# The fifth run of attention scores moved ahead of the output product, in a two-layer kernel on one core

## The chip, the cores and the metric

The kernel runs on one core of a Trainium2 chip. The core has a matrix engine (PE, with its weight loads PEld), a vector engine (DVE), an activation engine (ACT), a general engine (POOL), and a queue that issues transfers (SP). Each engine works through its own instructions in the order in which the program gives them, and semaphores hold an instruction back until what it needs is there. The metric is the time of one execution in microseconds (us), as the device measures it; lower is better.

## The reference, cut to what matters

There are 8 batches of 512 tokens with 256 channels. Each of two layers normalises its input and adds an attention and a feed-forward result to it. The change lies in the first layer's attention, which has 16 heads of 64 channels, rotated queries and keys, and a causal mask:

```python
q = (x @ Wq + bq).reshape(b, s, H, L)      # the same for k and v
q = _apply_rope(q, cos, sin)               # and k
scores = jnp.einsum('bnqd,bnkd->bnqk', q, k) / jnp.sqrt(jnp.float32(L))
scores = jnp.where(causal, scores, -1000000000.0)
attn = jax.nn.softmax(scores, axis=-1)
attended = jnp.einsum('bnqk,bnkd->bnqd', attn, v)
return attended @ Wo + bo
```

The first layer's feed-forward part is a product with eight-bit weights, the second layer an attention with a gate and a feed-forward part with a gate. The change does not touch them.

## The kernel before, in words

**Tiling.** One pass (`at`, 0 to 15) does the attention of eight heads of one batch, so a batch takes two passes: `b, g = divmod(at, 2)`. In this text an even pass has g = 0, an odd pass g = 1. The score matrix of a head is causal; it is cut into 16 strips of 32 query rows, and strip i needs 32 (i + 1) key columns. The strips are grouped into five runs (`RUNS`): run 0 has strips 15, 14 and 0; run 1 has 13, 1, 12, 2; run 2 has 11, 3, 10, 4; run 3 has 9, 5, 8, 6; run 4 has strip 7 alone. A strip pair fills 512 columns of a PSUM bank, and there is one bank for each of two sets of heads. All PSUM tiles come from one pool of eight banks that are given out in rotation.

**What one run goes through.** `scores(at, run)` (L463) makes the score matmuls on tiles of 64 rows by 32 columns of the array (L474). `soften` (L481) has DVE add the mask and take the maximum (L500) and ACT take the exponential with its sum (L504). `divide` (L510) takes reciprocals on DVE (L515) and scales the chances on POOL (L520). `turn` (L528) transposes the chances on DVE (L540). When all five runs are turned, `weigh` (L545) multiplies them with the values (L553) in the next pass, and `keep_weighed` (L561) has ACT copy the result out of PSUM (L567).

**What else a pass does.** `project(at, which)` computes rotated queries (which = 0) or keys (which = 1) of a later pass: matmuls into `pq` (L395) on the whole array, copied out by ACT with the bias (L400), half exchanged by SP's transfers (`y<-l`, L402); `turn_qk` (L405) rotates them later with two DVE products (L412) and a sum on POOL (L427). `project_v` (L429) computes values into `pv` (L437), which ACT copies out (L443) and SP stores. `finish(at - 1)` (L373) is the output product of the pass before, for two halves of the tokens: matmuls into `pw` (L357) on the whole array and an addition on DVE (L366). In even passes 2 to 12, `transpose_x(b + 1)` (L307) transposes the normalised input of the next batch on PE into `pxt` (L313), ACT copies it to `xnT` (L316), and SP stores `xnT` for later (`xnf`, L305) and then loads the input of a later batch (L80). The keys of `project(at + 2, 1)` in an even pass are made from just this new `xnT`. Passes 12 and 13 also do part of the feed-forward product of two batches (`add_quantised`, L193).

**What sets the order.** The order of the work is written out by hand (`manual_schedule`): every engine has its instructions in the order of the calls in the program. The calls of passes 1 to 13 around the change are these (L849 to L869), with the branches for single passes left out:

```python
scores(at, 3); soften(at, 3)
turn_qk(2 * at + 3, 0); turn(at, 2); divide(at, 3)
transpose_x(b + 1)           # even passes
finish(at - 1)
scores(at, 4); soften(at, 4)
turn(at, 3); project(at + 2, 1); divide(at, 4)
```

Behind them the next pass begins with its run 0, `turn(at, 4)` and `weigh(at)`. Pass 14 leaves the loop ahead of these lines.

## Time and profile before

| what | value |
| --- | --- |
| time, median of 3 runs | 960.23 us (958.95 to 961.5) |
| time of the profiled execution | 956.88 us |
| span of the profiled execution | 955.1 us |
| granted clock of PE | 0.996 |
| busy: PE, DVE, POOL, ACT | 98%, 83%, 59%, 55% |
| output product, `pw` (L357) | 512 matmuls, 114.3 us |
| keys, `pq` from `wk` (L395) | 256 matmuls, 116.0 us |
| all scores (L474) | 4096 matmuls, 147.0 us |
| exponential of strip 7 (128 x 256) | 32, 501 ns each |
| maximum of strip 7 (128 x 256) | 32, 417 ns each |
| copies `xnT<-pxt` | 16, 572 ns each |

The profile shows one execution. Rows of a timeline give the start and the duration in microseconds, the engine, the line, the operation, the output and the input by their names in the program, the shapes, and how many instructions were merged in the row; in brackets stands how long the engine had been idle, and what ended the wait. Matmuls are pipelined and their ends are modelled, so that starts are the safer reading. The chain of waits is followed back from the last instruction, so it shows what set the end. "issue" stands for time in which an engine waited for nothing that the profile shows.

### The profile page before, as it was taken

The page shows a single profiled execution, that of the slowest core. Times are in us where ns is not written, and L with a number is a line of the kernel's source. Part 1 is how long each engine was busy: PE and PEld are TensorE (multiplying, and loading weights), DVE is VectorE, ACT ScalarE, POOL GpSimd, SP SyncE. Part 2 cuts the span into 40 slices and gives each one's busy share as a digit, 9 for nine tenths or more (in the row PEclk, how much of TensorE's full clock was granted, in tenths as well). Part 3 has the DMA queues.
Part 4 walks back from the last instruction along what each step waited for, and adds up shares of the span by engine and source line. Part 5 has one row for each costly group of instructions (what it writes and reads, how often), then busy time and mean ns, then how long its engine had stood idle before and what let it go on. Part 6 is the DMA issues. An engine that isn't in the chain of part 4 may idle for free.

```text
span 955.1 us, 27426 instructions
## 1 busy us (share of the span) xinstructions
PE 933.0 (98%) x10491; PEld 595.1 (62%) x10491; DVE 788.4 (83%) x2429; ACT 529.7 (55%) x1480; POOL 563.9 (59%) x698
## 2 busy tenths in 40 slices
PE   9989999999999999999999999999999999999998
PEld 5436555656666575656565655665656677777776
DVE  4898988898799789978997898787989588888864
ACT  3565465656564656574656655555667335555553
POOL 3595775655664757556665665989776424444321
PEclk9999999999999999999999999999999999999999
DMA  7666354426443545254444435353344122221111
GB/s 216 182 177 174 98 128 139 122 73 141 145 107 96 125 131 133 69 135 128 118 109 129 121 89 156 112 156 90 91 123 124 46 76 67 71 69 51 34 33 34
DMA packets 60930, 105.40 MB, mean 110 GB/s; under 512 B 7552, under 2 KB 38272, under 8 KB 60800
## 3 DMA queue, kind: packets, MB, share of 16 engines
q1 hardware_dynamic: 58928, 102.01, 39.4%
q10 hardware_dynamic: 1872, 1.64, 0.7%
q8 instruction: 83, 1.36, 0.6%
q14 instruction: 47, 0.39, 0.1%
HBM read 39.14 MB, written 28.84 MB: 71 GB/s over the span
## 4 chain that ended last, share of the span: by engine, by line
PE 88%; DVE 5%; issue 2%; POOL 2%; ACT 2%; DMA 1%; SPq 0%; DVEq 0%; ACTq 0%; POOLq 0%
PE pq L395 21%; PE av L553 13%; PE sc L474 13%; PE pw L357 11%; PE pv L437 9%; PE po L713 6%; PE pk L660 3%; PE pg L675 3%; PE pvv L687 3%; PE c L632 2%; PE trc L700 1%; PE plr L234 1%; DVE t L540 1%; DVE p L500 1%; POOL h L427 1%
## 5 line engine op out<-in xcount | busy, mean ns | idle before, releaser
L504 ACT ACTIVATE p<-p,nm 128x64 f32<-128x64 f32 (+15 forms) x512 | 260.0, 511 | 154.4 <-DVE nm L500 124.4
L520 POOL TENSOR_SCALAR p<-p,rs 128x64 f32<-128x64 f32 (+15 forms) x512 | 270.1, 548 | 53.5 <-DVE rs L515 51.3
L427 POOL TENSOR_TENSOR h<-h,y 128x1024 f32<-128x1024 f32 x64 | 166.7, 2606 | 178.3 <-DVE y L412 97.0
L500 DVE CUSTOM_DVE_ANT_0 p<-sc,cmask 128x64 f32<-128x64 f32 (+15 forms) x512 | 191.1, 436 | 75.4 <-PE sc L474 74.9
L540 DVE STREAM_TRANSPOSE t<-p 128x256 f32<-128x256 f32 (+3 forms) x640 | 192.7, 367 | 20.7 <-POOL p L520 20.7
L474 PE MATMUL sc<-h,h 64*32 64x416 f32 (+15 forms) x4096 | 147.0, 398 | 9.0 <-issue 5.8
L474 PEld LDWEIGHTS sc<-h,h 64*32 64x32 f32 x4096 | 76.9, 107 | 95.6 <-issue 69.8
L553 PE MATMUL av<-t,vr 32*64 32x96 f32 (+15 forms) x4096 | 128.4, 394 | 2.9 <-issue 2.7
L553 PEld LDWEIGHTS av<-t,vr 32*64 32x64 f32 x4096 | 120.5, 131 | 10.3 <-issue 6.8
L395 PE MATMUL pq<-xnT,wk 128*128 128x512 f32 x256 | 116.0, 605 | 3.6 <-ACT xnT L316 3.6
L400 ACT ACTIVATE l<-pq,cs 128x512 f32<-128x512 f32 x128 | 84.5, 682 | 59.6 <-PE pq L395 54.5
L412 DVE TENSOR_TENSOR y<-y,cs 128x1024 f32<-128x1024 f32 x64 | 111.5, 1743 | 5.6 <-DMA y<-l 5.1
L395 PE MATMUL pq<-xnT,wq 128*128 128x512 f32 x256 | 114.5, 599 | 1.1 <-ACT att L567 0.9
L357 PE MATMUL pw<-wo,att 128*128 128x256 f32 x512 | 114.3, 381 | 0.0
L437 PE MATMUL pv<-wv,xnT 128*128 128x512 f32 x256 | 114.0, 598 | 0.0
L357 PEld LDWEIGHTS pw<-wo,att 128*128 128x128 f32 x512 | 96.0, 190 | 16.0 <-issue 3.7
L504 ACT ACTIVATION_READ_ACCUMULATOR p<-p,nm 128x1 f32 x512 | 96.8, 189 | 0.0
L395 PEld LDWEIGHTS pq<-xnT,wk 128*128 128x128 f32 x256 | 48.1, 192 | 65.0 <-issue 58.3
L437 PEld LDWEIGHTS pv<-wv,xnT 128*128 128x128 f32 x256 | 47.5, 190 | 57.9 <-issue 54.6
L395 PEld LDWEIGHTS pq<-xnT,wq 128*128 128x128 f32 x256 | 47.4, 190 | 56.8 <-issue 47.9
L412 DVE TENSOR_TENSOR h<-l,cs 128x1024 f32<-128x1024 f32 x64 | 78.7, 1230 | 4.3 <-ACT l L400 4.3
L567 ACT ACTIVATE att<-av,cs 128x512 f32<-128x512 f32 x64 | 38.7, 688 | 69.5 <-PE av L553 69.5
(111 smaller groups left out, 955.7 us busy)
## 6 DMA issues: line engine op xcount, KB each, us to landing
y<-l SPq DMA_DIRECT2D x256, 128.0 KB, 2.3
va<-v SPq DMA_DIRECT2D x32, 512.0 KB, 3.0
vr<-va SPq DMA_DIRECT2D x64, 256.0 KB, 4.5
x<-in_x SPq DMA_DIRECT2D x15, 512.0 KB, 4.5
xnf<-xnT SPq DMA_DIRECT2D x8, 512.0 KB, 3.0
x1f<-x SPq DMA_DIRECT2D x7, 512.0 KB, 3.6
out<-y SPq DMA_DIRECT2D x14, 256.0 KB, 2.2
cut_wo<-xnf SPq DMA_DIRECT2D x5, 512.0 KB, 4.5
```

The lines of the kernel that those rows point to most:

```text
L357: nc.tensor.matmul(pw[:, j, :], atts[at, p][:, tok], wo[:, 4 * (at % NH) + p, :], start=(p == 0), stop=(p == 3),)
L395: nc.tensor.matmul(pb, w[:, g, k, bass.ts(t, P)], xnT[b][:, k, :], start=(k == 0), stop=(k == NK - 1),)
L400: nc.scalar.activation(l[:, t, :], pb, AF.Identity, bias=cs[:, bias : bias + 1])
L412: nc.vector.tensor_tensor(dst, src, table[:, None, :].to_broadcast([P, 2, S]), ALU.mult)
L427: nc.gpsimd.tensor_tensor(h, h, y, ALU.add)
L437: nc.tensor.matmul(pb.rearrange("p (g n) -> p g n", g=2), xnT[b][:, k, bass.ts(2 * half + j, P)], wqkv[2][:, 2 * g : 2 * g + 2, k, :], sta ...
L474: nc.tensor.matmul(scored[at, i][e][j * Q : j * Q + Q, :], q[rows, j % 2, bass.ts(i, Q)], k[rows, j % 2, :n], start=True, stop=True,)
L500: nc.vector.tensor_tensor_reduce(p[:, e, col : col + n], sc, cmask[:, S - n :], -1.0 / L**0.5, BIG, ALU.add, ALU.min, nm[:, c : c + 1],)
L504: nc.scalar.activation(p[:, e, col : col + n], p[:, e, col : col + n], AF.Exp, bias=nm[:, c : c + 1], scale=-1.0, accum_out=sm[:, c : c + 1],)
L520: nc.gpsimd.tensor_scalar(p, p, rs[:, c : c + 1], 1.0, ALU.mult, ALU.mult)
L540: nc.vector.transpose(turned[at][c][:, :, at_ : at_ + (n - 1) * pitch(c) + 1 : pitch(c), :], p[:, :, c * P : c * P + n * Q].rearrange("p e ...
L553: nc.tensor.matmul(banks[j][e * L : e * L + L, i * Q :], vs[at][rows, m, c, bass.ts(e, L)], t[c][rows, e, m * pitch(c) + m : m * pitch(c) ...
```

## The change

Run 4 of the scores and its softmax are called ahead of the input's transposes and of the output product, directly behind what follows run 3. So on PE run 4 stands directly behind run 3, and the output product is followed by the keys. On DVE the two maxima of run 4 stand ahead of the two additions of the output product. On ACT the two exponentials of run 4 stand ahead of the two `xnT` copies in even passes. The order on POOL and SP stays. The change reaches passes 1 to 13.

```diff
@@ -851,6 +851,8 @@
             turn_qk(2 * at + 3, 0)
             turn(at, 2)
             divide(at, 3)
+            scores(at, 4)
+            soften(at, 4)
             if g == 0 and b < B - 1:
                 transpose_x(b + 1)
                 if b + 2 < B:
@@ -861,8 +863,6 @@
             finish(at - 1)
             if at == last - 2:
                 first_norm()
-            scores(at, 4)
-            soften(at, 4)
             turn(at, 3)
             if two:
                 project(at + 2, 1)
```

## The prediction

> **What bounds the kernel now.** I read the busy shares and the shares of the chain first, then the chain in order of time, then the timelines of PE, ACT and DVE around the moved step.

> The page's busy times and the chain's shares by engine:

> ```profile
> span 955.1 us, 27426 instructions
> ...
> PE 933.0 (98%) x10491; PEld 595.1 (62%) x10491; DVE 788.4 (83%) x2429; ACT 529.7 (55%) x1480; POOL 563.9 (59%) x698
> ...
> PE 88%; DVE 5%; issue 2%; POOL 2%; ACT 2%; DMA 1%; SPq 0%; DVEq 0%; ACTq 0%; POOLq 0%
> ```

> PE is busy for 98% of the span and carries 88% of the chain; the other engines have room on average (DVE 83%). So a gain is PE time saved in the loop, and a loss is anything that makes PE wait. Two stretches of PE's timeline, one odd pass (at = 3) and one even pass (at = 4); columns are start, duration, engine, line, operation, count:

> ```profile
> 196.90 1.96 PE L474 MATMUL sc<-h,h 64*32 64x320 f32 x64
> 198.78 7.17 PE L357 MATMUL pw<-wo,att 128*128 128x256 f32 x32
> 205.89 0.66 PE L474 MATMUL sc<-h,h 64*32 64x256 f32 x16
> 206.48 7.13 PE L395 MATMUL pq<-xnT,wk 128*128 128x512 f32 x16
> ```

> ```profile
> 241.84 1.96 PE L474 MATMUL sc<-h,h 64*32 64x320 f32 x64
> 243.72 1.09 PE L313 MATMUL pxt<-ident,x 128*128 128x128 f32 x8
> 244.66 7.07 PE L357 MATMUL pw<-wo,att 128*128 128x256 f32 x32
> 251.66 0.66 PE L474 MATMUL sc<-h,h 64*32 64x256 f32 x16
> 252.25 7.13 PE L395 MATMUL pq<-xnT,wk 128*128 128x512 f32 x16
> ```

> The reader sees no gap: each block starts where the one before it stops. I count a block from its start to the next block's start, since the ends are modelled: run 3 takes 1.89 (198.78 - 196.90, rounded), the output product pw 7.10 in the odd pass and 7.00 in the even one, run 4 0.59, the keys pq 7.06. Even passes alone transpose the next batch's input (pxt, 0.93), and their pq reads just that transposed input, xnT, which ACT copies out of PSUM. ACT and DVE in the same even pass:

> ```profile
> 247.57 1.04 ACT L316 COPY xnT<-pxt 128x512 f32<-128x512 f32 x2
> 252.97 0.51 ACT L504 ACTIVATE p<-p,nm 128x256 f32<-128x256 f32 x1 [4.35 <-DVE nm L500]
> ```

> ```profile
> 248.06 2.78 DVE L540 STREAM_TRANSPOSE t<-p 128x256 f32<-128x256 f32 x9
> 250.76 0.20 DVE L515 RECIPROCAL rs<-sm 128x4 f32<-128x4 f32 x2
> 250.88 0.66 DVE L366 TENSOR_TENSOR x<-pw,x 128x512 f32<-128x512 f32 x1
> ...
> 252.44 0.42 DVE L500 CUSTOM_DVE_ANT_0 p<-sc,cmask 128x256 f32<-128x256 f32 x1
> ```

> ACT now makes the two xnT copies at 247.57 and then idles 4.35 for DVE before run 4's exponentials. DVE has no gap between run 3's scores and the reciprocals at 250.76.

> **The change, part by part.** Nothing is added or removed; 16 score matmuls, two DVE maxima, two exponentials and their reads change place in 13 passes (at = 1 to 13). I write times as offsets from the start of run 3's scores.

> *PE, saving.* Run 4 now follows run 3. The trace holds this very pair once, after the loop, where 80 score matmuls stand together, from 703.10 to 705.42:

> ```profile
> 703.10 2.39 PE L474 MATMUL sc<-h,h 64*32 64x320 f32 x80
> 705.42 3.72 PE L357 MATMUL pw<-wo,att 128*128 128x256 f32 x16
> ```

> That is 2.32 against 1.89 + 0.59 = 2.48: 0.16 saved. A full-array block also pays at its edges with a tiled block (scores, av, c). Two rows of the chain in order of time have the same 16 matmuls, once between av and c, once between plr and trc:

> ```profile
> 758.77 3.65 PE pvv L687 x16
> ...
> 795.16 3.45 PE pvv L687 x16
> ```

> That is 0.20 for two edges, 0.10 for one; pw agrees (7.10 entered from scores, 7.00 entered from pxt). The change takes away pw's edge to run 4 and pq's edge from it: 0.20. A pass saves 0.16 + 0.20 = 0.36. Odd pass: 16.64 before, 2.32 + 7.00 + 6.96 = 16.28 after; a pq of 6.96 stands in the trace at 498.84, after a wait.

> [...]

> *Where the saving counts.* In at = 3, 5, 7, 9 and 11 PE waits for nothing behind the pq: the next weigh needs the first transpose of run 4's chances, which ends at +17.4 on DVE, and PE reaches it at 18.16. Those five give 5 x 0.36 = -1.8. In at = 1 and 13 DVE is late already: the next weigh starts at 124.71 with 1.64 of idle before it, and at 676.61, right behind the transpose that begins at 676.07; DVE's work is the same in sum, so these give 0. At 0 as the one end and 2 x 0.36 as the other, I take 0, by those rows.

> *ACT, the new wait.* The order of ACT is as written: run 4's two exponentials now stand ahead of the two xnT copies. They need DVE's maxima, and on DVE those stand behind run 3's maxima, the rotations (L412), the transposes of run 2 and the reciprocals; DVE comes free at +9.04 (250.88), in all of at = 2, 4, 6, 8, 10. From the maximum's start to its exponential is 0.53 (252.44 to 252.97), the two exponentials take 0.50 each from start to start (the second starts at 253.47), so the first copy starts at +10.57 instead of +5.73; a copy lasts 0.57, and 0.05 later PE can start. That step is seen in the first pass, where the copies stand behind exponentials (run 3's there) and the keys wait for them:

> ```profile
> 66.10 1.05 ACT L316 COPY xnT<-pxt 128x512 f32<-128x512 f32 x2
> 66.72 4.04 PE L395 MATMUL pq<-xnT,wk 128*128 128x512 f32 x5 [3.61 <-ACT xnT L316]
> ```

> So pq starts at 10.57 + 0.57 + 0.05 = 11.19. PE would have been ready at 2.32 + 0.93 + 6.90 = 10.15: a new idle of 1.04. Before, pq started at 10.41. So the pass is 0.78 later at pq, 0.68 after pq's lost edge. The second copy ends at 11.61 and is wanted at 12.05. What waits behind ACT's wait: these copies alone; pq's own evictions are not due before 12.9. At = 12 has 0.87 of extra PE work (acc) and DVE comes free at +9.73: pq at 11.87 against 11.29, +0.58, and +0.48 after the edge. Even passes: 5 x 0.68 + 0.48 = +3.9. Bounds of an even pass: -0.36 if the copies came in time; +0.78 if the edge is not saved. I take 0.68, since each term has its own row.

> *DVE, POOL, SP.* Run 4's maxima (0.69) go ahead of the two additions of the output product, which come 0.7 later; behind these stand the transposes of run 3, and in sum DVE does the same work. The 0.23 that DVE waits for pw goes; nobody was waiting for it. POOL's order is unchanged. SP's order too, but the store of xnT waits for the copies: it leaves at some 253.5 instead of 248.64, and the load of x (249.08) and the store of x1 (252.49) queue behind it. The exchange y<-l behind them is issued at 256.74 and is used by DVE at 264.2, so I cost it at nothing; without that cover 1.5 MB would stand before it. PSUM banks rotate: in even passes pw takes the bank of run 3's first scores, which DVE has read at +2.64, while pw starts at +3.25; covered by 0.6.

> *Sum.* -1.8 + 3.9 = +2.1. The profiled execution took 956.88 (span 955.1 and 1.8 around it), so 959.0; it lies 3.35 under the median of the runs, 960.23. On the median: 962.3, +0.22%.

> **The rivals.** *The copies come in time* (faster): all 11 passes that count save 0.36, -4.0, 956.3. For it speaks that the PE edges are sure; it decides if DVE reaches run 4 by +8.0 instead of +9.04. Against: +9.04 stands in five passes out of five, with DVE busy from +1.19 on.

> *No saving on PE*: the 0.36 is eaten, because DVE, free at +17.70 in odd passes against first scores ready at 17.83, becomes the bound when PE is earlier. Then even passes cost 5 x 0.78 + 0.58 = 4.5 and odd ones 0: 964.7. For: a slack of only 0.13 there. Against: DVE then waits 1.00 for PE before the next run 3.

> *Moved transfers collide*: the store, load and store of 512 KB each now end close to the weigh, where PE shows idle put down to "issue" (1.24, 1.03 and 1.96 at 639, 405 and 588), all in passes that start with loads of 512 KB and more. One more such idle of 0.6 in each of 6 even passes: +2.1 + 3.6 = 5.7, 965.9. Against: from issue to landing these take 3.0, 4.5 and 3.6 by the page's issues, so the burst should be over by some 260, and odd passes 5, 7, 9 and 11 start with none.

> That the order doesn't change is no rival: it is written out by hand.

> **How the numbers follow.** Sum as worked out 0.55, no saving 0.20, collision 0.12, copies in time 0.13. About 0.3% (2.9 us) is what a measurement of this kernel can tell from no change. The sum at +2.1 lies 0.8 inside that bound; half the spread of the runs (958.95 to 961.5) is 1.3, so about a quarter of this case goes above: 0.42 of its 0.55 inside, 0.13 above. Slower: 0.13 + 0.20 + 0.12 = 0.45; same 0.42; faster 0.13. The range leaves out the copies in time and the outer part of the collision: 958.5 to 966. The likeliest case's own range is 960.5 to 964.

> **What would show it.** Right: 80 score matmuls of 2.32 in each pass, odd passes of 16.28, in even passes a PE gap of about 1.0 before pq released by ACT's xnT, copies starting at +10.6. Wrong: copies before the exponentials, no gap before pq, odd passes of 16.64, or longer "issue" idles at the weigh.

## The result, and the profile after

The changed kernel takes 963.38 us (median; 959.6 to 965.26) where the kernel before takes 959.5 (955.69 to 961.5): a ratio of 1.0043, with a 95% interval of 1.0025 to 1.0061. A second comparison on another occasion gave 961.2 against 959.14, a ratio of 1.0029 (1.0011 to 1.0047). A ratio is estimated from all runs, so it is not exactly the quotient of the two medians; differences in microseconds below are the ratio's share of the time before, here +4.1 and +2.8. So the change costs some 3 to 4 us. The sum had said +2.1.

The page of the changed kernel, busy times and the chain's shares by engine:

```profile
span 963.3 us, 27428 instructions
...
PE 934.1 (97%) x10491; PEld 600.0 (62%) x10491; DVE 787.3 (82%) x2429; ACT 530.7 (55%) x1480; POOL 564.1 (59%) x698
...
PE 85%; DVE 6%; issue 3%; ACT 2%; POOL 2%; DMA 1%; SPq 0%; DVEq 0%; ACTq 0%; POOLq 0%
```

PE's busy time is what it was (934.1 against 933.0), its share of the chain fell from 88% to 85%, and "issue" and DVE each took one point more: PE waits more (29.2 us of the span without work, 22.1 before). This execution (965.06 with what lies around the span) is at the long end of its kernel's runs. What follows is therefore read by pass.

PE in the same two passes as before, first the odd one (at = 3), then the even one (at = 4); columns are start, duration, engine, line, operation, count, and in brackets idle time with what ended it:

```profile
200.43 2.39 PE L474 MATMUL sc<-h,h 64*32 64x320 f32 x80
202.75 7.17 PE L357 MATMUL pw<-wo,att 128*128 128x256 f32 x32
209.76 7.03 PE L395 MATMUL pq<-xnT,wk 128*128 128x512 f32 x16
216.72 1.09 PE L474 MATMUL sc<-h,h 64*32 64x512 f32 x16
```

```profile
245.30 2.39 PE L474 MATMUL sc<-h,h 64*32 64x320 f32 x80
247.62 1.09 PE L313 MATMUL pxt<-ident,x 128*128 128x128 f32 x8
248.55 7.07 PE L357 MATMUL pw<-wo,att 128*128 128x256 f32 x32
256.45 7.13 PE L395 MATMUL pq<-xnT,wk 128*128 128x512 f32 x16 [0.83 <-ACT xnT L316]
263.51 1.07 PE L474 MATMUL sc<-h,h 64*32 64x512 f32 x13
```

Run 3 and run 4 are one block of 80 matmuls, 2.32 long (202.75 - 200.43). From run 3 to the next run 0 the odd pass takes 216.72 - 200.43 = 16.29 instead of 16.64, the even pass 263.51 - 245.30 = 18.21 instead of 17.47. In the even pass the keys wait 0.83 for ACT's `xnT`, counted from the modelled end of the output product. ACT and DVE of that pass say why:

```profile
254.84 0.51 ACT L504 ACTIVATE p<-p,nm 128x256 f32<-128x256 f32 x1 [3.71 <-DVE nm L500]
...
255.34 0.49 ACT L504 ACTIVATE p<-p,nm 128x256 f32<-128x256 f32 x1
...
255.84 1.05 ACT L316 COPY xnT<-pxt 128x512 f32<-128x512 f32 x2
```

```profile
251.52 2.78 DVE L540 STREAM_TRANSPOSE t<-p 128x256 f32<-128x256 f32 x9
254.23 0.20 DVE L515 RECIPROCAL rs<-sm 128x4 f32<-128x4 f32 x2
254.34 0.39 DVE L500 CUSTOM_DVE_ANT_0 p<-sc,cmask 128x256 f32<-128x256 f32 x1
...
255.01 1.35 DVE L366 TENSOR_TENSOR x<-pw,x 128x512 f32<-128x512 f32 x2
```

ACT idles 3.71 for run 4's maximum with the finished transposes behind it in its queue, and makes the copies at 255.84, 10.54 behind run 3; before, they came at +5.73. The output product, which had hidden the copies until then, is over at about 255.6, and PE waits from there on.

To see where the time went in sum, I cut each trace at the weighs (the products with the values, early in each pass) and at run 3, and took means over three traces of the kernel before and four of the changed one (us):

| stretch | before | after | difference |
| --- | --- | --- | --- |
| start to pass 1's weigh | 77.79 | 77.37 | -0.4 |
| odd passes, run 3 to next run 0 (7) | 117.32 | 114.81 | -2.51 |
| even passes, run 3 to next run 0 (6) | 105.74 | 110.11 | +4.37 |
| next run 0 to the weigh (13) | 27.15 | 27.30 | +0.2 |
| weigh to run 3 (13) | 349.89 | 349.01 | -0.9 |
| from pass 14's weigh to PE's last matmul | 274.95 | 277.04 | +2.09 |

Rows two and three hardly vary: within 0.01 in each kernel's traces for the odd passes, within 0.3 for the even ones, and that spread is all pass 12. The stretches from the weigh to run 3 scatter more within one kernel (348.93 to 351.22 before, 347.74 to 350.38 after) than the two means differ, with idles that the profile puts down to "issue"; their difference says nothing. The last row is in no step of the prediction; it is taken up below.

### The profile page after: what moved, and what is told of

The parts are those of the page before. It is cut to its first block, busy times and chain, and to the rows that moved or that the text cites. A ratio compares the mean times of both kernels' runs of the same rounds, so it can differ in the third digit from the quotient of the medians.

```text
span 963.3 us, 27428 instructions
## 1 busy us (share of the span) xinstructions
PE 934.1 (97%) x10491; PEld 600.0 (62%) x10491; DVE 787.3 (82%) x2429; ACT 530.7 (55%) x1480; POOL 564.1 (59%) x698
## 3 DMA queue, kind: packets, MB, share of 16 engines
q10 hardware_dynamic: 1872, 1.64, 0.7%
## 4 chain that ended last, share of the span: by engine, by line
PE 85%; DVE 6%; issue 3%; ACT 2%; POOL 2%; DMA 1%; SPq 0%; DVEq 0%; ACTq 0%; POOLq 0%
PE pq L395 22%; PE av L553 13%; PE sc L474 12%; PE pv L437 9%; PE pw L357 7%; PE po L713 6%; PE pk L660 3%; PE pg L675 3%; PE pvv L687 3%; DVE p L500 2%; DVE t L540 2%; ACT p L504 2%; PE c L632 2%; PE plr L234 2%; PE trc L700 1%
## 5 line engine op out<-in xcount | busy, mean ns | idle before, releaser
L504 ACT ACTIVATE p<-p,nm 128x64 f32<-128x64 f32 (+15 forms) x512 | 260.0, 511 | 143.1 <-DVE nm L500 112.2
L500 DVE CUSTOM_DVE_ANT_0 p<-sc,cmask 128x64 f32<-128x64 f32 (+15 forms) x512 | 190.6, 435 | 83.8 <-PE sc L474 82.1
L540 DVE STREAM_TRANSPOSE t<-p 128x256 f32<-128x256 f32 (+3 forms) x640 | 192.6, 366 | 21.1 <-POOL p L520 21.1
L474 PE MATMUL sc<-h,h 64*32 64x416 f32 (+15 forms) x4096 | 144.3, 398 | 10.6 <-issue 7.4
L474 PEld LDWEIGHTS sc<-h,h 64*32 64x32 f32 x4096 | 79.2, 107 | 93.1 <-issue 67.8
L395 PE MATMUL pq<-xnT,wk 128*128 128x512 f32 x256 | 116.1, 606 | 8.4 <-ACT xnT L316 8.4
L412 DVE TENSOR_TENSOR y<-y,cs 128x1024 f32<-128x1024 f32 x64 | 111.1, 1736 | 6.3 <-DMA y<-l 5.8
L395 PE MATMUL pq<-xnT,wq 128*128 128x512 f32 x256 | 114.7, 600 | 0.2 <-ACT xnT L316 0.2
L357 PE MATMUL pw<-wo,att 128*128 128x256 f32 x512 | 114.3, 381 | 0.0
L357 PEld LDWEIGHTS pw<-wo,att 128*128 128x128 f32 x512 | 95.9, 190 | 16.4 <-issue 4.0
L504 ACT ACTIVATION_READ_ACCUMULATOR p<-p,nm 128x1 f32 x512 | 96.9, 189 | 0.0
L395 PEld LDWEIGHTS pq<-xnT,wk 128*128 128x128 f32 x256 | 49.0, 194 | 67.8 <-issue 51.4
L395 PEld LDWEIGHTS pq<-xnT,wq 128*128 128x128 f32 x256 | 47.4, 190 | 56.2 <-issue 47.6
L412 DVE TENSOR_TENSOR h<-l,cs 128x1024 f32<-128x1024 f32 x64 | 78.7, 1230 | 4.4 <-ACT l L400 4.4
```

Source lines behind the costliest of these rows:

```text
L357: nc.tensor.matmul(pw[:, j, :], atts[at, p][:, tok], wo[:, 4 * (at % NH) + p, :], start=(p == 0), stop=(p == 3),)
L395: nc.tensor.matmul(pb, w[:, g, k, bass.ts(t, P)], xnT[b][:, k, :], start=(k == 0), stop=(k == NK - 1),)
L412: nc.vector.tensor_tensor(dst, src, table[:, None, :].to_broadcast([P, 2, S]), ALU.mult)
L474: nc.tensor.matmul(scored[at, i][e][j * Q : j * Q + Q, :], q[rows, j % 2, bass.ts(i, Q)], k[rows, j % 2, :n], start=True, stop=True,)
L500: nc.vector.tensor_tensor_reduce(p[:, e, col : col + n], sc, cmask[:, S - n :], -1.0 / L**0.5, BIG, ALU.add, ALU.min, nm[:, c : c + 1],)
L504: nc.scalar.activation(p[:, e, col : col + n], p[:, e, col : col + n], AF.Exp, bias=nm[:, c : c + 1], scale=-1.0, accum_out=sm[:, c : c + 1],)
```

## The experiments

Theory: in-order ACT holds the copies back behind run 4's exponentials, which costs even passes 0.7 each, while PE saves 0.36 in each pass at its block edges. Rivals: PE saves nothing; or the transfers that move with the copies collide with other work.

### The changed kernel again, its two halves, and the copies put first

The changed kernel was run once more with three others on the same chip.

> The changed kernel once more, beside the kernel before on the same chip, so that the other runs of this call can be set against it. By the theory of the ACT order (six even passes each lose about 0.7, five odd passes each save 0.36) the loss is +2 to +4 us. By the rival that PE saves nothing it is about +4.7. By the rival of colliding transfers it is +5.7. In the trace, odd passes from run 3 to the next run 0 take 16.28 by the theory and 16.64 by the rival without a saving.

Measured: 1.0029 (1.0011 to 1.0047), +2.8 us; odd passes 16.29 as in the first trace. The saving isn't eaten behind them either: pass 3 takes 44.23 to 44.26 from its weigh to the next in all four traces of the changed kernel, and 44.59 to 44.60 in the three of the kernel before. The rival without a saving is out.

The next kernel moves the softmax behind the transposes, and leaves the score matmuls where the change put them:

```diff
             divide(at, 3)
             scores(at, 4)
-            soften(at, 4)
             if g == 0 and b < B - 1:
                 transpose_x(b + 1)
                 if b + 2 < B:
                     x_next.append(load_x(b + 2))
+            soften(at, 4)
```

> Run 4's score matmuls stay directly behind run 3, but its softmax is called behind the input's transposes, so that ACT makes the two xnT copies before run 4's exponentials. Nothing else moves. Theory (ACT order): the PE gap before the keys of even passes goes, even passes take 17.1 instead of 18.2 from run 3 to the next run 0, odd ones stay at 16.28, and the kernel is about 4 us faster than before (11 passes x 0.36), 6 to 8 us faster than the changed one. Rival without a PE saving: no faster than before, 0 to +0.5. Rival of colliding transfers: the store of xnT leaves early again, so the same gain as by the theory; it is told apart by the run with late transfers.

Measured: 953.51 against 959.14, a ratio of 0.9949 (0.9925 to 0.9973), -4.9 us. PE in its pass 4:

```profile
240.71 2.39 PE L474 MATMUL sc<-h,h 64*32 64x320 f32 x80
243.03 1.09 PE L313 MATMUL pxt<-ident,x 128*128 128x128 f32 x8
243.96 7.07 PE L357 MATMUL pw<-wo,att 128*128 128x256 f32 x32
250.87 7.03 PE L395 MATMUL pq<-xnT,wk 128*128 128x512 f32 x16
257.83 1.96 PE L474 MATMUL sc<-h,h 64*32 64x512 f32 x48
```

There is no wait, and the even pass takes 17.12: 0.36 under the 17.48 of before, and 1.09 under the changed kernel's 18.21. One call's place makes the difference between a loss and a gain. PE's waits in sum for the copies (total, times, longest), first in the changed kernel, then in this one:

```profile
PE pq L395 <- ACT xnT L316: 8.6, 8, 3.6
```

```profile
PE pq L395 <- ACT xnT L316: 3.9, 2, 3.6
```

The two waits that stay lie ahead of the loop. Six more, 4.7 us together, are the change's.

Odd and even passes alone, with the calls under `if g == 1` or `if g == 0` in the new place and under the opposite condition in the old one:

```diff
             divide(at, 3)
+            if g == 1:
+                scores(at, 4)
+                soften(at, 4)
...
-            scores(at, 4)
-            soften(at, 4)
+            if not (g == 1):
+                scores(at, 4)
+                soften(at, 4)
```

> Run 4 is moved in odd passes alone; even passes stay as before. Theory: 5 passes that save 0.36 and two (1 and 13) in which DVE is late already, so -1.8 us against before. If passes 1 and 13 save as well: -2.5. Rival without a PE saving: 0.

Measured: 0.9983 (0.9963 to 1.0004), -1.6 us: what the theory says, though the interval just reaches no change. The trace is clear: all seven odd passes are 0.36 shorter from run 3 to the next run 0, even ones as before.

> Run 4 is moved in even passes alone; odd passes stay as before. Theory: +3.9 to +4.3 us against before, a PE gap of about 0.9 before the keys of each even pass, and even passes of 18.2 from run 3 to the next run 0 against 17.47. Rival without a PE saving: about +4.5, nearly the same. Rival of colliding transfers: +6 and more, with longer idles put down to issue at the weigh behind even passes.

Measured: 1.0065 (1.0041 to 1.0089), +6.2 us (3.9 to 8.5). Even passes take 18.21 to 18.22 (18.92 in pass 12), 4.26 more in sum, as the theory has it. The measured 6.2 lies 2 above that. The rival of colliding transfers could claim those 2 us; so it was tried by itself.

### The transfers late, the scores alone, and the wait enlarged

The copies come first here, but the store of `xnT` and the load of `x` are issued as late as in the changed kernel. The diff is against the changed kernel:

```diff
                 nc.scalar.copy(xnT[b][:, k, :], pb)
-            if b > 0:
-                keep_input(b)
...
             scores(at, 4)
-            soften(at, 4)
             if g == 0 and b < B - 1:
                 transpose_x(b + 1)
-                if b + 2 < B:
-                    x_next.append(load_x(b + 2))
+            soften(at, 4)
...
             finish(at - 1)
+            if g == 0 and b < B - 1:
+                keep_input(b + 1)
+                if b + 2 < B:
+                    x_next.append(load_x(b + 2))
```

> As the run with the copies ahead of run 4's exponentials, but in even passes the store of xnT and the load of x are issued behind the output product's additions, at about +11.5 from run 3 as in the changed kernel, instead of +7. Theory (ACT order): they stay hidden, the time is that of the run with the copies first, -3 to -5 us against before. Rival of colliding transfers: about 0.6 lost in each even pass, so -1 us or slower, with longer idles at the weigh behind even passes.

Measured: 0.9955 (0.9937 to 0.9974), -4.3 us. In pass 4 the store leaves 11.5 behind run 3, in the changed kernel 11.6, with the copies first 6.8. The copies first were run beside it once more:

> The run with the copies ahead of run 4's exponentials once more, beside the two runs that it is compared with. Theory: -3 to -5.5 us against before, as in the first one (ratio 0.9949).

Measured: 951.96 against 957.29, a ratio of 0.9946 (0.9926 to 0.9966), -5.2 us. The two differ by less than their intervals, and even passes take 17.12 in both. The transfers are hidden either way; that rival falls.

The score matmuls alone in the new place, the softmax in the old one:

```diff
             divide(at, 3)
+            scores(at, 4)
             if g == 0 and b < B - 1:
                 transpose_x(b + 1)
...
-            scores(at, 4)
             soften(at, 4)
```

> Run 4's score matmuls alone are moved, directly behind run 3; its softmax stays where it was, behind the output product's additions. So PE has the order of the changed kernel, DVE and ACT that of the kernel before. Theory (the gain is PE's block edges alone): even passes 17.12 and odd ones 16.29 from run 3 to the next run 0, and the same gain as with the copies ahead of the exponentials, -3 to -5 us against before. If the earlier softmax had a share in that gain: less than this by that share.

Measured: 0.9963 (0.9948 to 0.9977), -3.5 us, even passes 17.12 and odd ones 16.29. So the gain is PE's, by the order of its blocks; an earlier softmax adds nothing that can be told apart.

The last kernel has PE's and DVE's order of before, and only ACT's copies behind run 4's exponentials, with the store and the load that follow them:

```diff
...
+            if b < 2:
+                copy_x(b, pbs)
+            return pbs
+
+        def copy_x(b, pbs):
+            for k, pb in enumerate(pbs):
                 nc.scalar.copy(xnT[b][:, k, :], pb)
             if b > 0:
                 keep_input(b)
...
             if g == 0 and b < B - 1:
-                transpose_x(b + 1)
-                if b + 2 < B:
-                    x_next.append(load_x(b + 2))
+                pbs = transpose_x(b + 1)
...
             soften(at, 4)
+            if g == 0 and b < B - 1:
+                copy_x(b + 1, pbs)
+                if b + 2 < B:
+                    x_next.append(load_x(b + 2))
             turn(at, 3)
```

> The kernel before with one thing moved: in even passes ACT makes the xnT copies behind run 4's exponentials. PE and DVE keep the order of before, so that run 4's maxima come at +10.6 (12.5 in pass 12) and the copies at about +12.1 (14.0). This takes the suspected wait alone and enlarges it. Theory (ACT order): the keys start at about +12.75 instead of +10.41 in passes 2 to 10 and at +14.6 instead of +11.3 in pass 12, so 5 x 2.3 + 3.3, about +15 us. If the wait were hidden or absorbed by later waits: well under that, +5 or less.

Measured: 979.89 against 957.29, a ratio of 1.0232 (1.021 to 1.0254), +22 us: the wait is real, is absorbed nowhere, and costs 7 more than its length. Keys of pass 2 and of pass 4 (the line numbers of this kernel are higher by 6), and the granted clock right behind the second one's start. It stands in a window's row behind the window, its length and the busy times of PE, PEld, DVE, ACT and POOL, as a share of full speed (0.69 is ACT's busy time, the clock is the 0.50):

```profile
163.88 7.13 PE L401 MATMUL pq<-xnT,wk 128*128 128x512 f32 x16 [2.25 <-ACT xnT L322]
```

```profile
257.45 8.83 PE L401 MATMUL pq<-xnT,wk 128*128 128x512 f32 x16 [2.26 <-ACT xnT L322]
```

```profile
258.40:261.80 3.40, 3.40 (x6) 1.32 (x5) 1.27 (x5) 0.69 (x1) 2.81 (x5) 0.50 0.86 284
```

They wait 2.25 and 2.26, as expected. In pass 2 the keys then take 7.13, in pass 4 8.83: the clock is halved for 3.4 us, and this adds 1.70 to the pass. Passes 4, 8 and 10 take 21.5 from run 3 to the next run 0, passes 2 and 6 19.8 (before: 17.48). So 5 x 2.32, 3 x 1.70 and 5.27 in pass 12 make 22.0.

### The clock at pass 15

The same halving explains the last row of the table above. Pass 15's scores wait 1.8 to 3.4 us for something that the profile doesn't show, in every trace. PE in the kernel before, then in the changed kernel's second trace:

```profile
731.36 1.08 PE L474 MATMUL sc<-h,h 64*32 64x352 f32 x28 [2.19 <-issue]
732.37 1.99 PE L234 MATMUL plr<-yt,crl 128*128 128x512 f32 x4
```

```profile
731.99 1.95 PE L474 MATMUL sc<-h,h 64*32 64x352 f32 x28 [2.57 <-issue]
733.87 2.72 PE L234 MATMUL plr<-yt,crl 128*128 128x512 f32 x4
```

The waits are much alike (2.19 and 2.57), but then 28 score matmuls take 1.95 instead of 1.08. The windows right behind, in the same order, have the clock at 1.00 and at 0.50:

```profile
731.40:734.80 3.40, 3.40 (x48) 1.50 (x55) 2.30 (x11) 2.92 (x13) 3.32 (x6) 1.00 0.63 140
```

```profile
732.00:735.40 3.40, 3.40 (x30) 1.48 (x31) 1.39 (x9) 1.68 (x9) 2.97 (x5) 0.50 0.57 117
```

Two more traces of each kernel were taken to see whether this is chance:

> The changed kernel, one more look. In all traces so far of kernels whose even passes wait (the changed one twice, even passes alone, copies behind), PE's idle at the scores of pass 15 is followed by 3.4 us at half the clock, and the work behind pass 14's weigh takes 276.7 to 277.8; in the six traces of kernels without that wait it takes 274.4 to 274.9 at full clock. If the half clock comes with the change, it is here again. If it is chance (how the idle falls against fixed stretches of 3.4 us), it may be missing.

> The kernel before, one more look at the same place. If the half clock at pass 15 comes with the change, it is not here (274.9 behind pass 14's weigh). If it is chance, it may be here (277).

> The changed kernel, a third look at the clock at pass 15; as in the first look.

> The kernel before, a third look at the clock at pass 15; as in the first look of the kernel before.

Measured: half clock at this place in both new traces of the changed kernel (276.85 and 276.62 behind pass 14's weigh), full clock in both of the kernel before (274.88 and 275.13). Over all traces it is there in the six of kernels with the wait in even passes (with even passes alone, too, where it could be the 2 us that were open), and missing in the eight without. So in the traces it came with the change each time, about +2.0 us at this place.

In the timed runs it doesn't add up to that. Each run has its mean granted clock on record, and one stretch of 3.41 us at half clock lowers it by 0.0018 (half of 3.41 in the span of 955.1). On the chip of the second comparison the mean over the runs is 0.9955 before (25 runs), 0.9952 in the changed kernel (12) and 0.9943 with even passes alone (6): about a fifth and two thirds of a stretch more, not a whole one. Half-clock stretches elsewhere, at pass 2's weigh and among pass 12's scores (126.90 and 594.53 in the changed kernel's first trace, 589.59 alone in the first one of the kernel before), come and go in the traces of both kernels, and the other rows of the table take some 1.1 back. Runs of equal granted clock in that comparison (0.993, 0.995 and 0.996) are 3.1, 2.6 and 1.6 us slower with the change, near the +2.1 of the sum.

## Why the prediction was right or wrong

**The direction and the range held**: slower, within 958.5 to 966. Slower had the largest chance (0.45), though the point lay inside 0.3% (0.42); the first comparison lies above that bound with 0.43%, the second at it with 0.29%, and both intervals contain it.

**PE, saving: right.** 16.28 was forecast for an odd pass, 16.29 measured; 2.32 for the merged scores in every pass.

**Where the saving counts: right, but for pass 1 perhaps.** Passes 5, 7, 9 and 11 keep it, and pass 3. Pass 13 gives it back, as forecast: from weigh to weigh it takes 47.1 to 47.2 before and 47.2 to 47.3 after, since DVE's transposes wait for POOL there: idles of 0.40 and 0.33 for the divided chances in the changed kernel, 0.97 and 0.34 with the copies first, against 0 and 0.35 before. Pass 1, also put at 0, takes 47.5 before and 46.8 after on average, but with a scatter of 1.2, so its 0.36 may well count.

**ACT, the new wait: right in mechanism, sized a little low.** Keys at +11.19 were forecast, +11.15 measured; copies at +10.57 and +10.54. The new wait is 0.99 from start to start (11.15 against 10.16 with the copies first), where 1.04 was forecast. But after it pq still took 7.06: the 0.10 that the sum had counted as saved, because pq no longer follows the scores, stayed. So +0.73 a pass instead of +0.68, and +0.55 to +0.82 in pass 12 instead of +0.48. Even passes: +4.37 instead of +3.9.

**DVE, POOL, SP: right.** The later transfers cost nothing (the run with late transfers). The additions no longer wait for pw and nobody gained from that.

**The sum: right in the loop, without a term for the clock.** The loop's rows give -2.51 + 4.37 = +1.86, and +2.2 with pass 13's 0.36 given back, which is the +2.1 of the sum, partly by luck: even passes cost 0.5 more than forecast, and pass 1 may have saved 0.36. The half clock behind a wait was priced at nothing: I counted idle time on PE at its own length. In the traces that is +2.0 at pass 15. The second comparison's +2.8 (1.1 to 4.5) agrees with +2.2 as it is; the first one's +4.1 (2.4 to 5.9) lies above it. Its runs of the changed kernel have a mean clock of 0.9933 against 0.9952 in the second, which is about one more half-clock stretch in a run; as the clocks of its runs before are not on record, it isn't shown that the clock makes the rest.

**The rivals.** Copies in time was the right counter-case, with the wrong condition: DVE needn't be earlier, the copies need only stand ahead in ACT's queue. That kernel, the change with one call moved, is, with the late transfers, the fastest here: 0.9946 and 0.9949 of before, where the sum's row for that case had -4.0 us and -4.9 and -5.2 were measured. No saving on PE is refuted by the odd passes' 16.29 together with pass 3, which keeps its 0.36 up to the next weigh; colliding transfers are refuted by the run with late transfers.

## What to carry to other kernels

When a call is moved for the sake of one engine, read every other in-order queue that it feeds: what waits behind its instructions there, and whose cover that eats. Split a step into its parts (matmuls, maxima, exponentials, copies) and place each by its own queue; here the matmuls' new place was worth 3.5 to 5 us, and the softmax's place ahead of the copies cost about 8 against the place behind them. And a wait on PE may cost more than its length: with the copies behind, the keys' wait of 2.26 us in pass 4 cost 1.70 more, the one of 2.25 in pass 2 nothing more.

## What the runs showed of the hardware

**Behind some waits of about 2 us PE's clock stood at half for 3.41 us, behind others as long it did not.** With the copies behind, the keys took 8.83 after a wait of 2.26 in pass 4, at a clock of 0.50, and 7.13 after one of 2.25 in pass 2. At pass 15 the clock was 1.00 after a wait of 2.19 in the kernel before, and 0.50 after one of 2.57 in the changed kernel's second trace.

Up to PE's last matmul the half clock starts at 67.35 and 589.59 in the first trace of the kernel before, and at 65.46, 126.90, 594.53 and 737.89 in the changed kernel's first; it lasts 3.41 each time, 6.83 at 65.46. In each of the two the starts lie whole multiples of one length apart: 522.24 is 153 x 3.4133; 61.44, 467.63 and 143.36 are 18, 137 and 42 x 3.4133. So I divided each trace into stretches of this length, placed so that the half clock starts where a stretch does, and took PE's idle time in each from 80 us on. These are all stretches of the two traces with more than 1.3 us of idle:

| trace | stretch | PE idle in it | clock in the next |
| --- | --- | --- | --- |
| before | 121.96:125.38 | 1.64 | 1.00 |
| before | 586.18:589.59 | 1.89 | 0.50 |
| before | 729.54:732.95 | 1.82 | 1.00 |
| after | 123.49:126.90 | 2.67 | 0.50 |
| after | 591.12:594.53 | 2.46 | 0.50 |
| after | 734.48:737.89 | 3.33 | 0.50 |

**Why the changed kernels' wait at pass 15 always fell into one stretch isn't settled.** In the six traces with the half clock a stretch began 8.5 to 9.4 us behind pass 15's weigh (9.31 in the changed kernel's first: 734.48 - 725.17), and the wait starts at 9.4; in the eight others one began at 9.8 to 10.6 (9.76 in the first of the kernel before: 729.54 - 719.78) and split it. What ties the place of the stretches to the kernels was not found.

**A block of full-array matmuls took about 0.10 us more for an edge to a block of tiled ones**, and the tiled block some 0.16 more for standing alone. In the odd pass, pw took 7.11 ahead of run 4 (205.89 - 198.78) and 7.01 ahead of the keys (209.76 - 202.75), the keys 7.06 behind run 4 and 6.96 behind pw, run 3 and run 4 together 2.48 in two blocks and 2.32 in one (202.75 - 200.43): 0.36 a pass (2.51 over the seven odd passes), the same to 0.02 in every trace with the new order, wherever the keys do not wait for the copies.
